# Order of the keys' products, of the layer norm's transposes and of the last ranks in a macaron block

## The chip, the cores and the metric

The kernel runs on one core of a Trainium2 chip. The metric is the time on the device in microseconds (us); the time before is the median of three runs. One further execution was profiled, and all durations, waits and places on the time axis come from it. TensorE is called PE, with its weight loads apart (PEld); VectorE is DVE, ScalarE is ACT, GpSimd is POOL and SyncE is SP.

## The reference

A macaron block on x of shape (2, 1024, 512), all in f32:

```python
x = x + 0.5 * ffn(layernorm(x))      # mixture of 2 experts, top-1 by a router
x = x + attention(layernorm(x))
x = x + 0.5 * ffn(layernorm(x))

def ffn(x):                          # per token: its expert's 512 -> 2048 -> 512
    h = x @ w_fc[e].T; a = square(where(h >= 0, h, 0.5 * h)); y = a @ w_proj[e].T
    # times the router's probability of the chosen expert
```

Attention has 16 heads with keys of 64, values of 128 and 64 slots each. q, k, v, s and a gate g are products of the normalised x with Wq, Wk, Wv, Ws, Wg; s is clipped to +-32. Two recurrences over the tokens keep a state of slots: the first gathers keys by exp(s) and is read by q, a softmax over the slots follows, and the second gathers values by the same weights and is read by that softmax. The result is normalised per head, multiplied with g times sigmoid(g), and goes through Wo.

## The kernel before, in words

**Stages.** The first mixture takes up to about 460 us; attention with its loop runs from about 500 to 1960 us, its last iterations together with the start of the second mixture; the second mixture ends the kernel. Tokens are sorted by expert through DRAM (`xs`): `Mixture.feed` (L248) takes one tile of 128 tokens, its moments and the router's value, and when a group is full (`LAST` groups of 4, 4, 4, 2, 1, 1 tiles in the second mixture) `rank` (L267) finds each token's place. A rank is a few small DVE operations (e L273, bef L280, r0 to pos L286 to L289), two matmuls rp (L282, L283), a square root and a reciprocal (L291, L292), and one indirect store per tile that POOL issues (L294).

**Attention** works on 64 units: for each of 2 batches, for each of 4 groups of 4 heads, 8 chunks of 128 tokens. The loop (L1294 to L1368) runs over i, with unit i as `cur`, i-1 as `mid` and i-2 as `old`. In an iteration stand in this order: steps of projections (keys and slots, values and gates) between the slots' scores of `mid` (ok), the transposes of `old`'s output (`to`), the softmax over the slots (its transposes `ts`, L1149), `transpose_u` (`tu`) and the key state of `mid`, the products for the value state, the transposes of `cur`'s keys and slots (`tk`), queries (pq), outputs (ov) of `mid`, scores (Ap) of `cur`, the output projection (po) of `old`, and the loads for a later group. After the output projection of the last head group the finished tile is fed to the second mixture.

`on_pe` (L947) chains all of these matmuls in the order in which they are written: each is issued after the one before (`att.pe`). The matmuls of the layer norm (ln, L206) and of the ranks (rp, L282 and L283) are not in that chain; the scheduler of the program places them where it finds them.

**Products.** Two neighbouring tiles are projected together by a scheme of seven products in place of eight, with sums of tokens (`X`, L970 to L974) and of weights. `keys_slots` (L1025) is such a generator, run in the even iterations. Its first step makes U (kU: keys' own bank in "pj") and copies it on ACT (kp, L1033), then C, one half of a second bank (kV), to which the key addition on DVE (k, L1052) adds kp. Its second step has the products V (the other half of kV) and U:

```python
            product(V, u.S[:, 0], T1, False)
            p5 = keep(V, "kv")
            product(U, u.S[:, 1], T2, False)
            u2 = keep(U, "ku")
```

`keep` copies a bank to SBUF on ACT. The third step adds a product to V again and forms the slots (E) from it and u2. The steps of `values_gates` (L977), U in "ok" and C, V in "pj", stand between them.

**The layer norm** of attention's input, `layernorm_T` (L185), is a generator over tiles of 128 tokens: load of the tile (xr, two buffers, shared with a copy u2 of `values_gates`; for batch 1 through SP), moments, normalisation on DVE (xr, L203), four transposes into the bank "tr" (one buffer, shared with `tk`, `tu` and `to`), a copy to xnT on ACT (L207), and one yield. In the loop, `next(norm)` is called for batch 0, head group 3 (L1347 and L1348), so that the eight tiles of batch 1 are normalised in iterations 24 to 31.

**Other queues.** POOL multiplies the gate (sg, L1217), forms sums of weights (L548 to L566 in the second mixture), and issues the scatters (L294, L648). SP issues the loads in order, wv (L180) and vgT (L914) among them.

Of the kernel before, what the change touches and what calls it, by code (L numbers as in the profile page):

```python
# [25 lines left out]
NG = H // HG  # L26
# [23 lines left out]
def tile_macaron(  # L50
# [134 lines left out]
    def layernorm_T(src, rows, xT, b, ph):  # L185
        for blk in range(2 * b, 2 * b + 2):
            xT[blk] = large_tile([P, DC, 512], f"xnT{ph}_{blk}")
            for j in range(4):
                nm = f"{ph}_{blk}_{j}"
                xn = work.tile([P, D], F32, tag="xr", name=f"xr{nm}")  # L190
                if b == 0:
                    x = rows[blk][:, j, 0:D]
                else:
                    x = xn
                    nc.sync.dma_start(out=x, in_=src[ts(x1_block(blk) * 4 + j, P), :])
                st = small.tile([P, 6], F32, tag="bnst", name=f"bnst{nm}")
                nc.vector.bn_stats(st, x)
                mv = small.tile([P, 2], F32, tag="mv", name=f"mv{nm}")
                nc.vector.bn_aggr(mv, st)
                rstd = small.tile([P, 1], F32, tag="rstd", name=f"rstd{nm}")  # L200
                nc.scalar.activation(rstd, mv[:, 1:2], AF.Sqrt, bias=eps)
                nc.vector.reciprocal(rstd, rstd)
                nc.vector.tensor_scalar(xn, x, mv[:, 0:1], rstd, ALU.subtract, ALU.mult)  # L203
                tp = ps1.tile([P, DC, P], F32, tag="tr", name=f"ln{nm}")
                for dc in range(DC):
                    nc.tensor.transpose(tp[:, dc, :], xn[:, ts(dc, P)], ident)  # L206
                nc.scalar.copy(xT[blk][:, :, ts(j, P)], tp)  # L207
                yield
# [23 lines left out]
    class Mixture:  # L232
# [3 lines left out]
        def __init__(self, ph, plan, split):  # L236
            self.ph, self.rows, self.split = ph, None, split
            self.passes, self.groups = plan
            self.starts = [sum(self.passes[:j]) for j in range(NPASS)]
            self.e1 = small_t([P, NT], "e1", f"e1{ph}")  # L240
            self.run = small_t([P, NT], "run", f"run{ph}")
            self.before = small_t([P, NT], "bef", f"bef{ph}")
            self.pos = small_t([P, NT], "pos", f"pos{ph}", mybir.dt.int32)

            self.own = small_t([P, NPASS], "own", f"own{ph}")
            self.seen = self.ranked = self.done = 0

        def feed(self):  # L250
            V, i = nc.vector, self.seen
            nm = f"{self.ph}_{i}"
            row = self.rows[i // 4][:, i % 4, :]
            st = small.tile([P, 6], F32, tag="bnst", name=f"bnst{nm}")
            V.bn_stats(st, row[:, 0:D])
            V.bn_aggr(row[:, D : D + 2], st)
            prod = work.tile([P, D], F32, tag="xr" if self.split else "sq", name=f"pr{nm}")
            V.scalar_tensor_tensor(
                prod, row[:, 0:D], row[:, D : D + 1], wd, ALU.subtract, ALU.mult,
                accum_out=row[:, D + 2 : D + 3],  # L260
            )
            self.seen += 1
            if self.seen == self.ranked + self.groups[self.done]:
                self.rank(self.groups[self.done])
                self.done += 1

# [673 lines left out]
    def attention(att, then, then_steps, weight_steps):  # L940
# [84 lines left out]
        def keys_slots(u):  # L1025
            pair = u, units[u.n + 1]
            B11, B21, B22, T1, T2, T3, T4 = att.ks[u.b, u.g]
            a11, a12, a21, a22 = halves(u)
            U = ps2.tile([P, 256], F32, tag="pj", name=f"kU{u.nm}")

            def keep(bank, tag):
                t = work.tile([P, 256], F32, tag=tag, name=f"{tag}{u.nm}", bufs=1)
                nc.scalar.copy(t, bank)  # L1033
                return t

            def key(v):
                v.k = work.tile([P, HG * DK], F32, tag="k", name=f"k{v.nm}")
                return v.k

            def slot(v, bank, other):  # L1040
                v.E = work.tile([P, HG * M], F32, tag="E", name=f"E{v.nm}", bufs=3)
                nc.vector.tensor_tensor(v.E, bank, other, ALU.add)
                nc.vector.tensor_scalar(v.E, v.E, -32.0, 32.0, ALU.max, ALU.min)
                nc.scalar.activation(v.E, v.E, AF.Exp)

            product(U, a11, B11, True)
            p1 = keep(U, "kp")

            bank = ps2.tile([P, 2, 256], F32, tag="pj", name=f"kV{u.nm}")
            C, V = bank[:, 0], bank[:, 1]  # L1050
            product(C, a12, B21, True)
            nc.vector.tensor_tensor(key(u), C, p1, ALU.add)  # L1052
            yield
            product(V, u.S[:, 0], T1, False)
            p5 = keep(V, "kv")
            product(U, u.S[:, 1], T2, False)
            u2 = keep(U, "ku")
            yield
            product(V, u.S[:, 3], B22, False)
            slot(u, V, u2)  # L1060
            yield
            product(U, u.S[:, 2], T3, False)
            slot(pair[1], U, p5)
            yield
            product(U, a22, T4, False)
            nc.scalar.copy(key(pair[1]), U)
            yield
# [78 lines left out]
        def slot_softmax(u):  # L1146
            tp = ps1.tile([P, HG, M], F32, tag="st", name=f"ts{u.nm}")
            for pr in range(NPR):
                on_pe(nc.tensor.transpose,   # L1149
                    tp[:, 2 * pr : 2 * pr + 2, :].rearrange("p h m -> p (h m)"), u.sT[:, pr, :], ident  # L1150
                )
            mx = small.tile([P, HG, 1], F32, tag="mx", name=f"mx{u.nm}")
            nc.vector.tensor_reduce(mx, tp, AX.X, ALU.max)
            u.u = work.tile([P, HG, M], F32, tag="e", name=f"e{u.nm}")
            nc.vector.tensor_tensor(u.u, tp, mx.to_broadcast([P, HG, M]), ALU.subtract)
            nc.scalar.activation(u.u, u.u, AF.Exp)  # L1156
            u.rs = small.tile([P, HG, 1], F32, tag="rs", name=f"rs{u.nm}")
            nc.vector.tensor_reduce(u.rs, u.u, AX.X, ALU.add)
            nc.vector.reciprocal(u.rs, u.rs)
# [19 lines left out]
        def transpose_u(u):  # L1179
            tp = ps1.tile([P, NPR, P], F32, tag="tr", name=f"tu{u.nm}")  # L1180
            for pr in range(NPR):
                on_pe(nc.tensor.transpose, 
                    tp[:, pr, :], u.u[:, 2 * pr : 2 * pr + 2, :].rearrange("p h m -> p (h m)"), ident
                )
            u.uT = work.tile([P, NPR, P], F32, tag="uT", name=f"uT{u.nm}")

            nc.vector.tensor_tensor(u.uT, tp, u.rC, ALU.mult)
# [106 lines left out]
        for i in range(n + 2):  # L1294
# [25 lines left out]
            if mid:  # L1320
                transpose_u(mid)
                update_key_state(mid)
            project("vk", "v")
            if mid:
                slot_weights(mid)
                value_state_products(mid)
# [17 lines left out]
            if old:  # L1344
                project_out(old)
            if cur:
                if cur.g == NG - 1 and cur.b == 0:  # L1347
                    next(norm)  # L1348
                if cur.g == 0 and cur.b and cur.c in (1, 2):
                    att.load_rows(2 * cur.b + cur.c - 1)  # L1350

                if cur.c >= 4 and cur.n + NC < n:
                    v = units[cur.n + NC]
                    if cur.c == 4:
                        att.load_queries(v.b, v.g)
                    elif cur.c == 5:
                        att.load_values_gates(v.b, v.g)
                    elif cur.c == 6:
                        att.load_keys_slots(v.b, v.g)
                    else:  # L1360
                        att.load_outputs(v.b, v.g)
                if cur.g == NG - 1 and cur.b == B - 1:
                    if cur.c == 1:
                        then.lead_pass()
                    elif cur.c >= 3:

                        with tc.issue_after(mid.gated.ins):
                            next(then_steps)  # L1368

    first_mixture = Mixture(0, FIRST, True)  # L1370
    last_mixture = Mixture(2, LAST, False)
# [7 lines left out]
    for ps, ck in ffn(first_mixture, x1_views):  # L1379
        if ps == NPASS - 1 and ck >= 2 and att.rows[ck - 2] is None:  # L1380
            att.load_rows(ck - 2)
        if ps == NPASS - 1 and ck == 3:
            with tc.issue_after(first_mixture.mark_dve.ins):
                next(norm, None)
            if (0, 0) not in att.vg:
                for load in (att.load_values_gates, att.load_keys_slots, att.load_queries, att.load_outputs):
                    load(0, 0)
# [56 lines left out]
```

## Time and profile before

| what | before |
|---|---|
| median of 3 runs | 2368.47 us (2363.77 to 2371.63) |
| profiled execution | 2368.13 us |
| its span | 2366.4 us |
| mean granted clock of TensorE | 0.992 |
| PE busy | 2270.1 us, 10552 matmuls |
| PEld busy | 1566.4 us |
| DVE busy | 1389.4 us |
| ACT busy | 782.9 us |
| POOL busy | 470.8 us |

A line of the timeline has the start in us, the duration in us, the engine, the line of the kernel, the operation, what it writes and reads, and how many were joined; in brackets stands how long the engine was idle before it, and what ended that. A line of the waits has the waiting engine, its tile and line, the releaser, then us in total, how many times and the longest. A line of the windows has the stretch, its length, and for each engine its busy time, then the granted clock of TensorE, the share of DMA and GB/s. Durations of overlapping matmuls do not add up; the distance of their starts does.

### The profile page before, as it was taken

What the parts mean: (1) busy time and instruction counts of PE and PEld (TensorE: products, weight loads), DVE (VectorE), ACT (ScalarE), POOL (GpSimd) and SP (SyncE); (2) the same over time, 40 slices, a digit from 0 to 9 for tenths busy, and PEclk for the clock granted to TensorE, in tenths of its full rate; (3) what the DMA queues carried; (4) which work ended last, traced back from release to release, by engine and by line L of the source; (5) the groups of instructions that cost most, each with busy time, mean ns of one, the idle gap of its engine ahead of it and who ended that gap; (6) DMA issues with size and microseconds to landing.
All of it is one profiled execution on the core that took longest, in us unless ns stands there. A gap on an engine that the chain in (4) does not pass through costs nothing.

```text
span 2366.4 us, 28341 instructions
## 1 busy us (share of the span) xinstructions
PE 2270.1 (96%) x10552; PEld 1566.4 (66%) x10552; DVE 1389.4 (59%) x3116; ACT 782.9 (33%) x1462; POOL 470.8 (20%) x401
## 2 busy tenths in 40 slices
PE   6999999999999999999999999999999989999998
PEld 5686787866656666665556666665665668888865
DVE  6553556557656656756666655655656666666411
ACT  2221222324334333343333343343433322222222
POOL 3613616101101101100101000000001244534000
PEclk9999999999999999999999999999999999999999
DMA  7516435221311411311301110111010104323442
GB/s 285 218 54 241 151 115 221 76 104 45 121 45 63 143 40 54 143 32 37 138 27 58 72 35 15 72 41 35 29 36 31 77 23 152 107 77 120 165 169 98
DMA packets 56938, 222.72 MB, mean 94 GB/s; under 512 B 5983, under 2 KB 13151, under 8 KB 38880
## 3 DMA queue, kind: packets, MB, share of 16 engines
q1 hardware_dynamic: 51232, 203.52, 24.1%
q0 software_dynamic: 5280, 16.85, 1.8%
q8 instruction: 84, 1.38, 0.2%
q14 instruction: 54, 0.44, 0.1%
q10 hardware_dynamic: 288, 0.52, 0.1%
HBM read 189.86 MB, written 31.54 MB: 94 GB/s over the span
## 4 chain that ended last, share of the span: by engine, by line
PE 75%; DVE 13%; issue 6%; ACT 2%; POOL 2%; DMA 1%; SPq 0%; POOLq 0%; DVEq 0%; ACTq 0%
PE U L949 9%; PE oa L673 6%; PE po L949 6%; PE hU L606 6%; PE pq L949 5%; PE o L673 5%; PE V L949 4%; PE kU L949 4%; PE hp L509 4%; PE kV L949 3%; PE hV L606 3%; PE op L728 3%; PE ov L949 3%; PE C L949 2%; DVE rC L1124 2%
## 5 line engine op out<-in xcount | busy, mean ns | idle before, releaser
L1217 POOL TENSOR_TENSOR sg<-sg,ms 128x512 f32<-128x512 f32 x64 | 67.6, 1056 | 1248.6 <-DVE ms L1215 1209.1
L949 PE MATMUL po<-wo,oT 128*128 128x512 f32 x512 | 238.4, 609 | 1.7 <-DVE A L1106 1.7
L949 PEld LDWEIGHTS po<-wo,oT 128*128 128x128 f32 x512 | 92.6, 191 | 102.4 <-issue 93.0
L509 PE MATMUL hp<-xsT,wfc 128*128 128x256 f32 (+1 forms) x768 | 149.8, 350 | 10.3 <-DMA wfc<-in_w_fc_dram 5.6
L509 PEld LDWEIGHTS hp<-xsT,wfc 128*128 128x128 f32 x768 | 128.0, 193 | 33.6 <-issue 13.9
L728 PE MATMUL op<-wp,a 128*128 128x512 f32 x320 | 143.2, 593 | 0.0
L1213 ACT ACT_TABLE_LOAD x64 | 82.1, 1283 | 157.1 <-DVE ms L1212 157.0
L496 DVE SCALAR_TENSOR_TENSOR t<-hp,r 128x256 f32<-128x256 f32 (+1 forms) x96 | 36.3, 378 | 153.7 <-ACT r L495 151.7
L949 PE MATMUL U<-vgT,X 128*128 128x512 f32 x256 | 120.3, 592 | 0.0
L949 PE MATMUL pq<-xnT,wq 128*128 128x512 f32 x256 | 112.5, 592 | 0.0
L1124 DVE RECIPROCAL rC<-CT 128x256 f32<-128x256 f32 x64 | 111.4, 1740 | 0.6
L606 PE MATMUL hU<-xsT,wfc 128*128 128x256 f32 x384 | 100.2, 383 | 0.9 <-ACT e L613 0.9
L728 PEld LDWEIGHTS op<-wp,a 128*128 128x128 f32 x320 | 59.7, 190 | 60.9 <-issue 57.4
L1106 DVE TENSOR_TENSOR A<-Ap,causal 128x256 f32<-128x256 f32 x128 | 53.1, 420 | 54.6 <-PE Ap L949 53.1
L495 ACT ACTIVATE r<-hp 128x256 f32<-128x256 f32 (+1 forms) x96 | 33.3, 348 | 155.3 <-PE hp L509 151.0
L949 PEld LDWEIGHTS pq<-xnT,wq 128*128 128x128 f32 x256 | 47.4, 190 | 53.6 <-issue 53.6
L606 PEld LDWEIGHTS hU<-xsT,wfc 128*128 128x128 f32 x384 | 72.2, 191 | 14.2 <-issue 3.0
L1156 ACT ACT_TABLE_LOAD x63 | 80.8, 1283 | 1.2
L949 PEld LDWEIGHTS U<-vgT,X 128*128 128x128 f32 x256 | 48.6, 190 | 47.6 <-issue 45.9
L995 ACT ACTIVATE th<-sg 128x512 f32<-128x512 f32 x64 | 40.4, 631 | 109.4 <-DVE sg L993 102.4
L1219 DVE TENSOR_TENSOR og<-ov,sg 128x512 f32<-128x512 f32 x64 | 44.2, 690 | 52.0 <-POOL sg L1217 52.0
L1248 ACT ACTIVATE oT<-to,gnh 128x512 f32<-128x512 f32 x64 | 44.0, 687 | 92.4 <-PE to L949 80.7
(296 smaller groups left out, 5087.8 us busy)
## 6 DMA issues: line engine op xcount, KB each, us to landing
wfc<-in_w_fc_dram SPq DMA_DIRECT2D x48, 1024.0 KB, 5.6
wp<-in_w_proj_dram SPq DMA_DIRECT2D x48, 1024.0 KB, 6.9
vgT<-vgs SPq DMA_DIRECT2D x16, 1024.0 KB, 5.3
wv<-in_w_v_dram SPq DMA_DIRECT2D x8, 1024.0 KB, 7.7
ksT<-kss SPq DMA_DIRECT2D x8, 1024.0 KB, 4.9
wo<-in_w_o_dram SPq DMA_DIRECT2D x8, 1024.0 KB, 4.8
xs<-xs SPq DMA_DIRECT2D x6, 1032.0 KB
wks<-in_w_ks_dram SPq DMA_DIRECT2D x24, 256.0 KB, 4.2
```

What stands on the lines that cost most here:

```text
L509: m.mark = nc.tensor.matmul(hp, lhsT=wfc[:, dc * HQ + hc * P : dc * HQ + (hc + 1) * P], rhs=xT[:, dc, :], start=(dc == 0), stop=(dc == DC ...
L606: m.mark = nc.tensor.matmul(bank, lhsT=left[:, d, :], rhs=right[:, d, :], start=start and d == 0, stop=d == 1, skip_group_check=True,)
L673: nc.tensor.matmul(bank[:, t, :], lhsT=left(q)[:, ts(t, P)], rhs=right(q), start=first and q == 0 and (t == 0 or last), stop=last and q == ...
L728: nc.tensor.matmul(ops[j], lhsT=a[hc][:, ts(j, P)], rhs=wp[:, ts(hc, D)], start=(ck == 0 and hc == 0), stop=(ck == NHQ - 1 and hc == HQ // ...
L949: att.pe = op(*args, **kw)
L1106: nc.vector.tensor_tensor(m[:, ts(j, NPR), :], pp, causal[:, 0:NPR, :], ALU.mult)
L1124: nc.vector.reciprocal(u.rC, u.CT)
L1156: nc.scalar.activation(u.u, u.u, AF.Exp)
L1213: nc.scalar.activation(ms, ms, AF.Sqrt, bias=eps, scale=1.0 / DV)
L1217: u.gated = then.gated = nc.gpsimd.tensor_tensor(sg, sg, ms.to_broadcast([P, HG, DV]), ALU.mult)
L1219: nc.vector.tensor_tensor(u.og, op, sg, ALU.mult)
L1248: nc.scalar.activation(u.oT, tp, AF.Copy, scale=gnh)
```

## The change

Four things are changed.

- In the second step of `keys_slots` the product U with its copy ku now stands ahead of V with its copy kv.
- `layernorm_T` gets a second yield between normalisation and transposes. In the loop, after the output projection, the transposes of the tile before are issued behind the last matmul of attention's chain, and then the next tile is normalised (iterations 24 to 31; the last transposes in iteration 32). Ahead of attention one more `next` is called.
- The second mixture's ranks are `deferred`: `feed` no longer ranks, and `settle` does it in each iteration of the loop, (right after `project("vk", "v")`), also behind the last matmul of the chain. After the loop `settle` is called once more.
- Two calls of `on_pe` are broken over lines.

```diff
@@ layernorm_T
                 nc.vector.tensor_scalar(xn, x, mv[:, 0:1], rstd, ALU.subtract, ALU.mult)
+                yield
                 tp = ps1.tile([P, DC, P], F32, tag="tr", name=f"ln{nm}")
@@ class Mixture, __init__
             self.seen = self.ranked = self.done = 0
+            self.deferred = not split
@@ feed
             self.seen += 1
-            if self.seen == self.ranked + self.groups[self.done]:
+            if not self.deferred:
+                self.settle()
+
+        def settle(self):
+            while self.done < len(self.groups) and self.seen >= self.ranked + self.groups[self.done]:
                 self.rank(self.groups[self.done])
                 self.done += 1
@@ keys_slots
             yield
+            product(U, u.S[:, 1], T2, False)
+            u2 = keep(U, "ku")
             product(V, u.S[:, 0], T1, False)
             p5 = keep(V, "kv")
-            product(U, u.S[:, 1], T2, False)
-            u2 = keep(U, "ku")
             yield
@@ the loop of attention
             project("vk", "v")
+            with tc.issue_after(att.pe.ins):
+                then.settle()
             if mid:
                 slot_weights(mid)
@@
             if cur:
-                if cur.g == NG - 1 and cur.b == 0:
+                if (cur.b, cur.g) == (0, NG - 1) and cur.c or (cur.b, cur.g, cur.c) == (1, 0, 0):
+                    with tc.issue_after(att.pe.ins):
+                        next(norm)
+                if (cur.b, cur.g) == (0, NG - 1):
                     next(norm)
@@ after the loop
+        then.settle()
@@ ahead of attention, in the last pass of the first mixture
             with tc.issue_after(first_mixture.mark_dve.ins):
+                next(norm, None)
                 next(norm, None)
```

More of the change, by code (lines that the diff above doesn't have):

```diff
@@ L1148, in slot_softmax @@
             for pr in range(NPR):
-                on_pe(nc.tensor.transpose,
+                on_pe(
+                    nc.tensor.transpose,
                     tp[:, 2 * pr : 2 * pr + 2, :].rearrange("p h m -> p (h m)"), u.sT[:, pr, :], ident
@@ L1181, in transpose_u @@
             for pr in range(NPR):
-                on_pe(nc.tensor.transpose,
+                on_pe(
+                    nc.tensor.transpose,
                     tp[:, pr, :], u.u[:, 2 * pr : 2 * pr + 2, :].rearrange("p h m -> p (h m)"), ident
```

## The prediction

> **What bounds the kernel now.** I read the page first: the share of each engine, and the chain that ended last.
>
> ```profile
> PE 2270.1 (96%) x10552; PEld 1566.4 (66%) x10552; DVE 1389.4 (59%) x3116; ACT 782.9 (33%) x1462; POOL 470.8 (20%) x401
> ...
> PE 75%; DVE 13%; issue 6%; ACT 2%; POOL 2%; DMA 1%; SPq 0%; POOLq 0%; DVEq 0%; ACTq 0%
> ```
>
> TensorE is the bound, and the change neither adds nor removes a matmul. It can only move the idle time of PE, so the next view is what PE waited for, in attention above all.
>
> ```profile
> PE rp L282 <- DVE e L273: 17.2, 4, 12.6
> PE kV L949 <- DVE k L1052: 14.0, 21, 1.8
> ...
> PE hC L606 <- DVE e L1155: 6.3, 1, 6.3
> ```
>
> The second row is the keys' V product waiting for the key addition. Of the first row 12.6 us is the first mixture's start, which the change leaves alone. The timeline of one even iteration shows the wait in place:
>
> ```profile
> 630.17 0.41 DVE L1052 TENSOR_TENSOR k<-kV,kp 128x256 f32<-128x256 f32 x1
> ...
> 630.64 0.73 PEld L949 LDWEIGHTS kV<-ksT,X 128*128 128x128 f32 x4 [0.78 <-DVE k L1052]
> 630.64 1.13 PE L949 MATMUL kV<-ksT,X 128*128 128x256 f32 x4 [0.53 <-DVE k L1052]
> ...
> 631.61 1.03 PE L949 MATMUL kU<-ksT,X 128*128 128x256 f32 x4
> 631.81 0.37 ACT L1033 COPY kv<-kV 128x256 f32<-128x256 f32 x1 [3.37 <-PE kV L949]
> ...
> 632.47 0.60 PE L949 MATMUL to<-ident,og 128*128 128x128 f32 x4
> ...
> 632.91 0.38 PE L949 MATMUL ts<-ident,sT 128*128 128x128 f32 x2
> ...
> 633.13 1.03 PE L949 MATMUL kV<-wks,X 128*128 128x256 f32 x4
> ```
>
> V (630.64) shares a bank with C, which the addition reads, so it waits until 630.58. The kU product at 631.61 needs nothing from that addition. Next come the places where the layer norm's and the rank's own matmuls stand in PE's order:
>
> ```profile
> 1077.67 0.66 PE L206 MATMUL ln<-ident,xr 128*128 128x128 f32 x4 [0.86 <-DVE xr L203]
> ...
> 1079.00 0.65 PE L949 MATMUL to<-ident,og 128*128 128x128 f32 x4 [0.68 <-ACT xnT L207]
> ```
>
> ```profile
> 1098.29 1.13 PE L949 MATMUL kV<-ksT,X 128*128 128x256 f32 x4 [1.78 <-DVE k L1052]
> ```
>
> ```profile
> 1845.49 0.39 PE L282 MATMUL rp<-e,strict 128*128 128x4 f32 x2 [1.61 <-DVE e L273]
> ```
>
> Here PE waits for the normalised tile, then for the bank "tr" that ln, tk, tu and to share, then for a key addition that stands on DVE behind the norm, and for a rank. All are waits in a chain that has no slack.
>
> **Keys' U ahead of V.** In the trace a 256-column matmul starts 216 ns after the one before it, so U's four take 864 ns. I measured from the last ok<-A,E matmul to the first matmul of `to`. With no wait (iterations 10, 18, 42, 50, 58) it is 2.033 us; in 17 other even iterations between 4 and 56 it is 2.51 to 2.80, because V starts 0.68 to 0.97 after that matmul instead of 0.20. The 17 excesses add to 10.4 us. U's 864 ns covers each of them whole, so they vanish. What is late next is V's third step at 633.13, which needs the kv copy. Now U and `to`, `ts` stand between: 945 ns of slack. Afterwards only `to` and `ts` do (4 and 2 transposes of 108 ns, 648 ns): slack 945 - 864 = 81 ns. The trace has a near row: U<-vgT,xnT starts with its releaser done 84 to 86 ns before and loses 79 ns, while with 183 ns nothing is lost. Behind it on PE stands the whole chain. I take 79 ns in 28 pairs, 2.2 us (bounds 0 and 28 x 0.37, one more ACT copy). In pair 0 no `to` and `ts` stand there, and V's third step waits about what V waited before (0.75), so it counts nothing. Sum: 10.4 - 2.2 = **8.2 us**.
>
> **Layer norm's transposes.** The distance of iterations (tk to tk) repeats with a period of eight: 19.65, 25.43, 19.22, 19.00, 20.76, 25.87, 20.68, 19.00 us. Over that pattern units 25 to 32, where a tile of batch 1 is normalised in each, are longer by 0.44, 0.94, 2.42, 2.08, 1.98, 2.87, 2.42, 2.15: 15.3 us. Afterwards the tile is normalised an iteration ahead and its four transposes follow the output projection: no wait for DVE, `tr` free. The transposes stay, 4 x 108 + 58 ns = 0.49 us each, 3.9 us for eight. The pattern itself holds V waits of 0.60, 0.66 and 0.66 for pairs 28, 30 and 32 that U removes too: +1.9. The key addition is still late behind the norm on DVE there: V waited 1.95 us in pairs 28 and 32, minus 0.86 leaves about 1.1 us over the three. V's third step costs 0.3. Sum 15.3 - 3.9 + 1.9 - 1.1 - 0.3 = **11.9 us**. The norm's first stage on DVE (bn_stats, xr, 0.54 us each) is only moved; its cover is the 41% of DVE that is idle, and exposed it would cost 8 x about 1.4 us (bn_stats 0.69, its sum-up 0.16, xr 0.54). The new orderings chain matmuls of PE among themselves, which it runs in order anyway, so they add no wait by themselves.
>
> **Ranks.** Deferred until after the step that contains V, two rp matmuls and their wait leave the place ahead of V. Rank at iteration 34: its unit is 21.53 against 19.22, 2.3 us, of which bef/rp work and a smaller wait stay; I take **1.0**. Iteration 62: 24.55 against 21.1 us, and 0.6 of V's regular wait; less 1.5 that stays, **2.5**. In iteration 60 PE waited 1.94 us ahead of the second mixture's lt, behind the same addition; U fills 0.87 of it, and with the third step's share I take **1.3**.
>
> Here a rule speaks about these stalls. After each, the granted clock fell:
>
> ```profile
> 1847.50:1850.50 3.00, 3.00 (x12) 2.52 (x12) 0.64 (x4) 0.48 (x2) 1.51 (x2) 0.50 0.11 40
> ```
>
> The 0.50 is the granted clock. It stood 3.41 us after stalls of 1.8 to 2.1 us at 1792, 1845 and 1881, costing 1.7 us each, but not after two of 1.95 at 1098 and 1204. The Trainium skill (TensorE: Matmul & The Clock Gate, "Why this matters for your kernels") wants no idle gap over about 3 us: by it such stalls cost no clock and shortening them returns only themselves. By the row two of them return 1.7 more each. I count the one at 1847 within iteration 62 and leave the other for the low end.
>
> **The tail.** After the loop's ranks, POOL runs weight sums without a gap, and a DVE operation sits through them:
>
> ```profile
> 1898.68 7.30 DVE L498 SCALAR_TENSOR_TENSOR t_1b<-hB 128x512 f32<-128x512 f32 x1
> ```
>
> ```profile
> 1899.30 1.27 POOL L551 TENSOR_TENSOR wfc<-wfc 128x512 f32<-128x512 f32 x1
> ```
>
> ```profile
> 1906.46 1.19 PE L606 MATMUL hC<-xsT,wfc 128*128 128x256 f32 x2 [6.32 <-DVE e L1155]
> ```
>
> Ordinarily t_1b takes 0.68. The rule in SBUF — State Buffer ("SBUF: two separate sides") is that a DVE operation with two SBUF inputs and a GpSimd one exclude each other for one whole instruction. That would be one POOL sum, 1.27 us; the row has five back to back, 6.6 us more. I take the row. Deferring the ranks moves their scatters (L294) past these sums, so the train is the same eight sums closed up, ending about 2.4 us earlier. Half-clock time after it (10.24 us) may shrink. Bounds: -2 (both scatters of rank 12, 0.99 us each, in the path) to +5 (most of the 6.32); I take **1.7**, nearer the train's 2.4. The last ranks' scatters stand ahead of other sums on POOL; those waited 10.4 us for PE before, more than a scatter (0.99 us), so nothing is charged.
>
> **Sum.** 8.2 + 11.9 + 1.0 + 2.5 + 1.3 + 1.7 = 26.6 us. From the profiled execution, 2368.13 (span 2366.4), this is 2341.5; it lies 0.3 under the median of runs, 2368.47. I say **2341**.
>
> **Rivals.**
> *Keys' gain given back.* The 81 ns of V's third step rest on ACT copying kv at once. If one more ACT operation like the ku copy (372 ns) comes between, V's third step waits 0.37 - 0.08 = 0.29 more in 28 pairs, 8.1 us: 2350. For it: nothing else stands between. Against: ACT is busy 33%, and ku is copied before V ends. Chance 0.17.
> *Clock and tail return more.* The half clock at 1793 and part of the 10.24 us go (1.7 + 3 to 5 us): 2334. For it, the three rows above; against, the two stalls that cost nothing. Chance 0.15.
> *It doesn't do what it says*: the waits move whole to the next operation, for DVE's work is the same and the additions come no earlier. Within 3 us of before, 2366. Against: iterations without the wait run 2.033, so nothing else stops them. Chance 0.05.
> *Slower: loads held on SP.* SP issues in order. The x tiles of batch 1 (xr) now wait for their buffer's transposes an iteration later, and two of them stand ahead of the loads of wv and vgT, issued at 1117.64, 1127.95 and 1134.02. I expect those at about 1143, and U<-wv needs them at 1167.63; with 7 to 8 us to land, 17 us are left. A hold of d costs d - 17: one iteration of 21.5 more gives 4.5, two 26, and it decides against the change from d = 44. At three, 64.5 us, the time is 2341 + 47 = 2388. Nothing I see holds them more than one. Chance 0.03.
>
> **How the numbers follow.** The sum as worked has 0.60, around 2341. The low end, 2334, takes in the clock case; the high end, 2351, the gain given back. The last two cases, 0.08, and some spread lie outside. A measurement of this kernel can tell 0.3%, 7 us, from no change: below 2361 is faster. Only the fourth case is the same, only the fifth slower. Faster 0.94, same 0.03, slower 0.03.
>
> **What would show it.** Right: kV<-k waits all but gone from the PE rows, with the step from ok<-A,E to `to` at 2.0 to 2.1 us in regular pairs; ln waits gone, units 25 to 32 within 0.7 us of the pattern; rp after V with waits under 1 us in 34 and 62. Wrong: a new row kV<-kv with 0.3 us or more each; ln or lt waiting for `tr`; U<-wv or U<-vgT waiting for a DMA; an hC or hV wait in the tail longer than 6.3.

## The result and the profile after

The changed kernel takes 2335.56 us (median of four runs, 2334.97 to 2335.80) against 2369.09 of the kernel before in the same comparison: a ratio of 0.9861, with a 95% interval of 0.9844 to 0.9878. Its profiled execution has a span of 2334.1 us, 32.3 less than before, and a mean granted clock of 0.996. From the page, busy times and the chain:

```profile
PE 2260.4 (97%) x10552; PEld 1560.6 (67%) x10552; DVE 1386.8 (59%) x3116; ACT 781.2 (33%) x1462; POOL 471.8 (20%) x401
...
PE 80%; DVE 10%; issue 5%; DMA 2%; ACT 1%; POOL 1%; SPq 0%; POOLq 0%; another core or an unknown queue 0%; DVEq 0%; ACTq 0%
```

The same matmuls have a larger share of a shorter chain, and DVE's share fell from 13% to 10%. What PE waited for now (total, times, longest):

```profile
PE rp L288 <- DVE e L279: 12.8, 1, 12.8
...
PE to L955 <- DVE og L1227: 3.6, 4, 2.1
...
PE kV L955 <- DVE k L1058: 3.2, 6, 0.8
```

Of rp only the first mixture's start is left; V's wait fell from 14.0 us in 21 places to 3.2 in 6. The wait of `to` for og grew from 1.0 us in 2 places to 3.6 in 4, up to 2.1 us long. The timeline of the iteration shown before:

```profile
629.94 1.13 PE L955 MATMUL kU<-ksT,X 128*128 128x256 f32 x4
630.06 0.41 DVE L1058 TENSOR_TENSOR k<-kV,kp 128x256 f32<-128x256 f32 x1
...
630.91 1.03 PE L955 MATMUL kV<-ksT,X 128*128 128x256 f32 x4
...
631.97 0.37 ACT L1039 COPY kv<-kV 128x256 f32<-128x256 f32 x1 [0.49 <-PE kV L955]
...
632.42 1.10 PE L955 MATMUL kV<-wks,X 128*128 128x256 f32 x4
```

U runs while the addition ends, and V follows without a wait. V's third step (the last row) starts 80 ns after the kv copy ends (632.34), about the 81 ns foreseen.

To see where 32.3 us come from I laid both traces side by side, by the distance of each iteration's first tk transpose to the next. "Tail" is what follows the last of them:

| place | foreseen gain, us | measured, us |
|---|---|---|
| regular iterations 1 to 24 and 35 to 59 | 8.2 | 9.7 |
| iterations 25 to 33, beside the layer norm | 11.9 | 5.6 |
| iteration 34 | 1.0 | 0.8 |
| iteration 60 | 1.3 | 0.0 |
| iteration 62 | 2.5 | 3.4 |
| tail | 1.7 | 13.1 |
| up to the first tk | 0 | -0.3 |
| sum | 26.6 | 32.3 |

The sum is near, but two terms are far off in opposite directions: that they nearly cancel is luck. They are what the experiments are for. Each group of the norm's transposes now stands where the prediction put it, right behind the output projection and without a wait:

```profile
1063.93 3.70 PE L955 MATMUL po<-wo,oT 128*128 128x512 f32 x8
1067.46 0.60 PE L207 MATMUL ln<-ident,xr 128*128 128x128 f32 x4
```

Nevertheless iteration 31 is longer than before, 23.99 us against 21.42, though it has no rank and no norm wait. The timeline of POOL there, and then PE's:

```profile
1154.12 0.96 POOL L300 DMA_INDIRECT xs<-x,pos  x1 [0.30 <-issue]
1155.09 0.20 POOL L142 COPY x<-toki 128x4 int32<-128x4 int32 x1
1161.47 0.19 POOL L142 COPY x<-toki 128x4 int32<-128x4 int32 x1 [6.18 <-DMA xs<-x,pos]
1161.61 1.03 POOL L1225 TENSOR_TENSOR sg<-sg,ms 128x512 f32<-128x512 f32 x1
```

```profile
1163.52 0.63 PE L955 MATMUL to<-ident,og 128*128 128x128 f32 x4 [2.12 <-DVE og L1227]
```

Behind the deferred rank's scatters on POOL stand two copies of token numbers into row tiles. The second copy waits 6.18 us for the scatters to land, and the gate's multiplication sg stands behind it; og and `to` follow. The order on POOL was the same before, but there scatters and copies were done nine microseconds ahead of the next gate:

```profile
1155.56 1.04 POOL L294 DMA_INDIRECT xs<-x,pos  x1 [0.30 <-issue]
1160.06 0.32 POOL L142 COPY x<-toki 128x4 int32<-128x4 int32 x2 [3.46 <-PE kU L949]
1169.63 1.04 POOL L1217 TENSOR_TENSOR sg<-sg,ms 128x512 f32<-128x512 f32 x1 [9.25 <-DVE ms L1215]
```

Deferred, the scatters have moved up against the gate, which starts 12.0 us after the iteration's first tk in place of 8.5. The windows show what the clock does then (last columns: granted clock, DMA share, GB/s):

```profile
1161.20:1164.40 3.20, 0.82 (x5) 0.42 (x4) 1.72 (x5) 0.23 (x2) 1.18 (x2) 1.00 0.60 190
1164.60:1167.80 3.20, 3.20 (x6) 1.65 (x7) 3.10 (x9) 2.12 (x3) 0.00 (x0) 0.50 0.31 120
```

In the tail the DVE operation that had taken 7.30 us is short. Before, it began (1898.68) in the issue of a scatter with five sums behind it; now the rank's first scatter is issued after the last sum. The first row is of before, the others are of after:

```profile
1898.28 0.99 POOL L294 DMA_INDIRECT xs<-x,pos  x1 [0.30 <-issue]
```

```profile
1876.25 1.75 DVE L504 SCALAR_TENSOR_TENSOR t_1b<-hB 128x512 f32<-128x512 f32 x1
```

```profile
1885.18 1.02 POOL L300 DMA_INDIRECT xs<-x,pos  x1
```

```profile
1879.62 1.10 PE L612 MATMUL hV<-T,S 128*128 128x256 f32 x4 [2.35 <-DVE hA L644]
```

The last row is PE's longest wait there; it stands in place of the 6.32 us for hC.

### The profile page after: what moved, and what is told of

It is laid out like the page before. It is cut to its first block, busy times and chain, and to the rows that moved or that the text cites. A ratio compares the mean times of both kernels' runs of the same rounds, so it can differ in the third digit from the quotient of the medians.

```text
span 2334.1 us, 28356 instructions
## 1 busy us (share of the span) xinstructions
PE 2260.4 (97%) x10552; PEld 1560.6 (67%) x10552; DVE 1386.8 (59%) x3116; ACT 781.2 (33%) x1462; POOL 471.8 (20%) x401
## 4 chain that ended last, share of the span: by engine, by line
PE 80%; DVE 10%; issue 5%; DMA 2%; ACT 1%; POOL 1%; SPq 0%; POOLq 0%; another core or an unknown queue 0%; DVEq 0%; ACTq 0%
PE U L955 9%; PE po L955 8%; PE oa L679 6%; PE hU L612 6%; PE V L955 5%; PE pq L955 5%; PE o L679 5%; PE kU L955 4%; PE kV L955 4%; PE ov L955 4%; PE hV L612 3%; PE hp L515 3%; PE op L734 3%; PE C L955 3%; PE ok L955 2%
```

## The experiments

**Theory** after the result: keys and norm bring what the waits say. The tail comes from the fourth rank's two scatters leaving the train of POOL's sums, so that t_1b no longer sits through it. The loss in iteration 31 is POOL held by the copies. **Rival**: the tail is shorter only because everything ends earlier and the half-clock stretches fall elsewhere; and the loss in 25 to 33 comes from the norm's moved stage on DVE. The clock records of the traces give the time at half clock. Work there takes twice as long: in the stretch at 1792.91 us of the kernel before, 256-column matmuls start 427 ns apart in place of 216. A stretch thus costs about half its length, and less where PE waits in it (iteration 60 lost 1.44 us to one of 3.41). "Span less clock" below is the span minus half of the time at half clock, and a gain "less clock" is worked out from it. For the kernel before it is 2366.4 - 39.65 / 2 = 2346.6, for the changed one 2334.1 - 21.32 / 2 = 2323.4: 9.2 us of the 32.3 are clock.

**Keys alone.** From the changed kernel, the norm's split and the deferral undone:

```diff
-            self.deferred = not split
+            self.deferred = False
...
                 nc.vector.tensor_scalar(xn, x, mv[:, 0:1], rstd, ALU.subtract, ALU.mult)
-                yield
...
-                    with tc.issue_after(att.pe.ins):
-                        next(norm)
```

> Only U ahead of V in the keys' second step; the norm's transposes and the ranks stand as before. Theory: of the 32 us, the order of the products gives 9.7 in regular pairs and some 2 to 3 in the pairs beside the layer norm (V stalls of 1.95 us less U's 0.86); the tail behind the last iteration is left as it was, because what shortens it is that the ranks' scatters leave POOL: 2368 - 12.5 = about 2356. Rival: the tail gets shorter merely because the loop ends at another time and the half-clock stretches fall elsewhere; then this alone shortens the tail too, towards 2345.

Measured: 2349.85 us, ratio 0.9930 (0.9907 to 0.9953). Regular iterations gained 9.5 us, 25 to 33 only 1.1, the tail 3.3. Less clock, the span fell by 14.9, the tail by 1.8. The median lies between the two expectations; the tail's stall is unchanged (t_1b 7.30 us), so the rival is not borne out by the trace, but the clock moved by 4.9 us in this one execution, 1.5 of them in the tail. Iteration 34 gained 0.7 and iteration 62 2.4, with their ranks where they were.

**Norm alone.** The order of keys' products and the deferral undone:

```diff
-            self.deferred = not split
+            self.deferred = False
...
-            product(U, u.S[:, 1], T2, False)
-            u2 = keep(U, "ku")
             product(V, u.S[:, 0], T1, False)
             p5 = keep(V, "kv")
+            product(U, u.S[:, 1], T2, False)
+            u2 = keep(U, "ku")
```

> Only the layer norm's transposes behind the output projection. Theory: iterations 25 to 32 lose 15.3 us over the regular pattern, 3.9 of it are the transposes themselves and about 2 are waits of V behind the key addition that stay: about 9 less, 2359, with no half-clock stretch at 1164 us, since no rank holds POOL there. Rival: the norm's moved stage on DVE is what made these iterations gain only 5.6 us with the whole change: then about 2363.

Measured: 2354.05 us, ratio 0.9957 (0.9943 to 0.9971). Iterations 25 to 33 gained 5.3, with 31 shorter by 1.98 and no half clock at 1164. Two other half-clock stretches appeared, at 1144 us in this part and at 1233 us in iteration 34, each about 1.7 us of cost; the ones that iterations 60 and 62 had before did not come, and these gained 1.4 and 1.7 though nothing in them was changed. Less clock the span fell by 8.9, about the 9 expected; the median is 5 us under the 2359 expected.

**Ranks alone.** Keys and norm undone, the deferral left.

```diff
                 nc.vector.tensor_scalar(xn, x, mv[:, 0:1], rstd, ALU.subtract, ALU.mult)
-                yield
...
-            product(U, u.S[:, 1], T2, False)
-            u2 = keep(U, "ku")
             product(V, u.S[:, 0], T1, False)
             p5 = keep(V, "kv")
+            product(U, u.S[:, 1], T2, False)
+            u2 = keep(U, "ku")
```

> Only the ranks deferred. Theory: the tail gains about 13 us (the DVE operation t_1b no longer sits through five POOL sums, and the half-clock stretches that follow go), iteration 62 gains 3.4, iteration 31 loses 2.6 since the four scatters and the copies behind them hold POOL while the gate waits: 2368 - 14 = about 2354. Rival (tail by chance of time): tail within 2 us of before, 2366.

Measured: 2359.70 us, ratio 0.9976 (0.9969 to 0.9983), between the theory's 2354 and the rival's 2366. The tail gained 11.4, iteration 62 2.7; iteration 31 lost 4.6 and iteration 34 1.7, each with a half-clock stretch. Less clock the whole gain is 4.8 us, that of the tail 6.0. t_1b took 1.75 us. The tail's rival is out: with the loop no shorter than before, the tail is shorter all the same.

**Keys and norm, ranks as before.**

```diff
-            self.deferred = not split
+            self.deferred = False
```

> The whole change without deferred ranks. Theory: the tail is as before, iteration 31 has no wait for the gate: 2368 - 12.5 - 8.5 = about 2347. Rival (tail by chance of time): the tail shorter here too, 2336 or less.

Measured: 2339.17 us, ratio 0.9887 (0.9867 to 0.9907): not the 2347 of the theory, nor the rival's 2336. The sizes were off: with both changes iterations 25 to 33 gained 10.1, more than the 6.4 of the two alone (1.7 of the difference are the stretch at 1144 us), iteration 60 1.4 and 62 2.4. The tail gained 3.8, of which 3.3 are clock. Its stall stood as before:

```profile
1869.93 7.29 DVE L504 SCALAR_TENSOR_TENSOR t_1b<-hB 128x512 f32<-128x512 f32 x1
```

So the deferral on top of the other two brought little (ratio 0.9861 against 0.9887, with intervals that overlap): in the traces its tail is shorter by 9.2 us (5.1 less clock), and its iteration 31 longer by 4.6.

**The changed kernel again**, as a mark.

> The changed kernel once more, as the mark for the three others: about 2335.6. The half-clock stretches of 3.41 us lie on a grid of 3.413 us whose phase no kernel sets; if they follow from where a stall falls on that grid, some of them stand elsewhere in this execution, or are missing, with the same waits.

Measured: 2333.44 us, ratio 0.9857 (0.9841 to 0.9872). `to` waited 1.71 us for og in iteration 31, and this time no half-clock stretch followed: 21.91 us in place of 23.99. One appeared at 1877.6 instead. Of the 2.1 us between the two, 0.4 are the wait and the rest the clock. Part of what two executions of one kernel differ by is thus where a stall falls on the clock's grid.

**Only late ranks deferred**, from iteration 40 on, by a line at the head of the loop:

```diff
-            self.deferred = not split
+            self.deferred = False
...
+            then.deferred = i >= n // 2 + NC
```

> Ranks deferred only from iteration 40 on, so that the first two stand as before the change and the later ones as after it. Theory: the wait of `to` for og in iteration 31 (2.1 us, and the half clock behind it) goes, since POOL's scatters come early again and the gate doesn't wait behind the copies; the tail keeps what it gained: 4 to 5 us less than the changed kernel, about 2331. Rival (the stall comes from the norm's moved stage, not from POOL): no difference, 2335.5.

Measured: 2329.96 us, ratio 0.9836 (0.9823 to 0.9849); iterations 25 to 33 gained 10.1 over the kernel before, the wait for og is gone. That is 3.5 us under the changed kernel beside it, though the intervals overlap. The rival, the norm's stage, is out: it stands here as in the changed kernel, and the wait is gone.

**Only the scatters late.** Ranks computed in their old places; from the third on their scatters are issued at the deferred place.

```diff
+            if self.hold:
+                self.held.append(scatter)
+            else:
+                scatter()
...
+            then.hold = i >= n // 2 + NC
...
-                then.settle()
+                then.release()
```

> Ranks computed where they stood before the change, matmuls included; only the scatters of the third rank and later are issued at the deferred place. Keys and norm as changed. Theory: what shortens the tail is the two scatters leaving the train of POOL's sums, so t_1b takes about 1.7 us in place of 7.3 and the tail is 8 to 9 us shorter than with keys and norm alone: about 2330. Rival: the rp matmuls' place on PE does it; then t_1b takes 7.3 and the time is 2339.

Measured: 2336.24 us, ratio 0.9867 (0.9852 to 0.9883), not 2330. No DVE operation sat through the train any more, yet PE waited in the next place:

```profile
1874.76 1.34 PE L623 MATMUL hV<-xsT,S 128*128 128x256 f32 x4 [2.99 <-DVE hB L648]
```

hB waited behind three Q sums on DVE, each lengthened by a wait for one POOL sum (1.23 to 1.48 in place of 0.41). The tail, less clock, is 2.9 us shorter than before, against 6.1 with late ranks deferred whole and 0.6 with keys and norm alone. In these single traces the scatters' place thus explains about half of the tail's gain; the other half came only when the rank's small operations and matmuls moved too. Why was not taken apart further.

**Copies late.** The changed kernel, with the two copies held behind the gate of the iteration:

```diff
-                    att.load_rows(2 * cur.b + cur.c - 1)
+                    with tc.issue_after(mid.gated.ins):
+                        att.load_rows(2 * cur.b + cur.c - 1)
```

> The changed kernel with the two copies of token numbers held behind the gate's multiplication on POOL. Theory: what held POOL at 1155 to 1161 us was the second copy, waiting for the scatters to land; four scatters of 1.26 us remain and end before the gate is ready: `to` waits 0 to 0.5 us in iteration 31, 4 to 5 us less than the changed kernel, about 2331. Rival: the scatters themselves hold POOL; less than 1.5 us gained.

Measured: 2331.24 us, ratio 0.9845 (0.9830 to 0.9859). That is 2.2 us under the changed kernel beside it, not 4 to 5, and the intervals overlap. In the trace the gate runs 3.5 us earlier in its iteration, 8.5 us after the first tk as before the change:

```profile
1157.56 1.04 POOL L1225 TENSOR_TENSOR sg<-sg,ms 128x512 f32<-128x512 f32 x1 [3.04 <-DVE ms L1223]
```

It no longer waits for POOL, and iteration 31 is 19.44 us, against 23.99 and 21.91 in the two executions of the changed kernel. PE has no wait for og left in this stretch; what remains between 1035 and 1240 us is V's:

```profile
PE kV L955 <- DVE k L1058: 2.8, 5, 0.8
```

The copy, not the scatters themselves, held the gate.

**The feed an iteration later**, on top of the last two versions:

```diff
             if u.g == NG - 1:
-                then.feed()
+                if u.b:
+                    then.feed()
+                else:
+                    due.append(u)
@@ behind the second project("k", "v")
+            while due:
+                due.pop()
+                then.feed()
```

> The changed kernel, the copies late on POOL, and for batch 0 the feed of a finished tile to the second mixture moved into the next iteration, behind the step with U, so that the router's product (pr, 0.74 us on DVE) stands behind the key addition. Theory: the V waits of 0.63 to 0.98 us that stay in iterations 26 to 34 come from pr and its aggregate standing ahead of the key addition; five of them go, 3 to 3.5 us less than with the copies alone: about 2328. Rival: og, not pr, sets when the addition starts; less than 1 us.

> Ranks deferred only from iteration 40 on, with the same move of the feed. The early ranks' matmuls stand ahead of V in iterations 30 and 34 and now come after a later pr: V's waits in 26, 28, 32 go (about 2 us), those in 30 and 34 stay or grow by up to 0.9 each: 2328 to 2330. Which of the two is the faster says whether the first two ranks are better deferred, once the copies and the key addition are out of the way.

Measured: 2332.15 us, ratio 0.9848 (0.9835 to 0.9860), and 2333.50 us, 0.9850 (0.9837 to 0.9864). Neither is below the version without the move (0.9845 and 0.9836), and in the second's trace iterations 25 to 33 are 1.0 us longer. The trace of the first tells why: in 28, 32 and 34 moments and pr still stood ahead of the key addition on DVE, since a place in the program binds only where an order is written; only in iteration 30 does V start earlier (0.31 us late in place of 0.71). The question was not put by these kernels.

**The feed bound behind the key addition.**

```diff
-            nc.vector.tensor_tensor(key(u), C, p1, ALU.add)
+            att.added = nc.vector.tensor_tensor(key(u), C, p1, ALU.add)
@@ behind the second project("k", "v")
...
+                with tc.issue_after(att.added.ins):
+                    then.feed()
```

> As the version with the copies late on POOL, and the whole feed of a finished tile (moments and router product) held behind the key addition on DVE, which the move into the next iteration alone had not done in 26, 28 and 32. Theory: V's waits of 0.63 to 0.98 us in the even iterations 26 to 34 go, since without moments and pr the addition starts at least 0.7 us earlier: 3 us less than with the copies alone. Rival: og, which waits for POOL, still stands ahead and sets the addition's start; less than 1 us.

> The mark beside it: the changed kernel with the copies late, about 2331, with V's waits of 0.63 to 0.98 us in iterations 26 to 34 as before.

Measured: 2328.14 us, ratio 0.9839 (0.9826 to 0.9852), beside 2329.52, 0.9850 (0.9836 to 0.9863), of the mark. In the trace four of the five waits are gone. Iteration 26, which has no feed ahead of it and waits behind og, keeps 0.68, and 34 has a new wait, for the kv copy:

```profile
PE kV L955 <- DVE k L1058: 0.5, 1, 0.5
PE kV L955 <- ACT kv L1039: 0.3, 1, 0.3
```

Iterations 25 to 34 are 2.7 us shorter than in the mark. At the medians the difference is 1.4 us, and the intervals overlap, so the runs do not separate these two versions. Against the changed kernel (0.9857 and 0.9861) the version with the bound feed, at 0.9839, has the lower ratio, as the one with late ranks has (0.9836); these intervals overlap too, while the traces show iteration 31 in each shorter than in the two executions of the changed kernel, by 4.6 and by 2.5 us.

## Why the prediction was right, and where only its sum was

The forecast of faster, and the range, held; the median lies 5.4 us under the predicted 2341, near the low end. That the sum came so near is in part luck: 9.2 of the 32.3 us are clock, most of it not in the sum, and a term 6.3 us too high stands beside one 11.4 too low. One sign that the prediction named failed: units 25 to 32 were to lie within 0.7 us of the pattern, and 31 lies 5.0 above. By its own steps:

- **Keys' U ahead of V**: the mechanism and both sizes hold. Each waiting pair gained its excess less 75 to 80 ns, as the 81 ns of slack told; a pair without a wait lost 70 to 80 ns (iterations 10 and 18: 19.22 to 19.29). The term was 8.2 and measured 9.7: I had left pair 24 out (0.69) and charged V's third step in 28 pairs, where this part has 23; pair 42 lost another wait of 0.3.
- **Layer norm's transposes**: waits gone as foreseen, 0.4 to 0.5 us per tile of transposes paid. The step that failed is "leaves about 1.1 us over the three": V starts 0.63, 0.71 and 0.63 us late in 28, 30 and 32 (2.0 in all), with 0.69 in 26 and 0.98 in 34, because the key addition stands behind og and the router's product. (The row of 2.8 us in 5 places counts only PE's idle part.) The size was a slip of mine too: 1.95 less 0.86 is 1.1 in each of two pairs, 2.2 over both. The version with the bound feed shows that all but the one in 26 come from the feed (moments and pr), which I had not put into the sum.
- **Ranks, scatters**: "so nothing is charged" failed. I had looked only at POOL's queue in the tail, and not at the first rank, where the scatters and the copies that wait for their landing stand ahead of the gate: 4.6 us in iteration 31 with the half clock after it, 2.5 in the execution without. Copies late and late ranks both took it back. This and V's waits are the gap between 11.9 and 5.6.
- **Iterations 34 and 62**: near in size (1.0 and 2.5 foreseen, 0.8 and 3.4 measured), but I had credited both to the deferral and, in 62, to the clock. Keys alone, with the ranks in place, already gains 0.7 in 34. In 62 norm alone gains 1.7 because no half clock came; less this, keys alone gains 0.7 and ranks alone 1.0.
- **Iteration 60**: 1.3 foreseen, 0.0 measured. The first wait of lt fell from 1.94 us (before, the first row) to 0.88, as worked out, but U no longer stands between the groups of lt, and those now wait for ACT's copy of the group before:

```profile
1792.44 0.71 PE L482 MATMUL lt<-ident,xn 128*128 128x128 f32 x4 [1.94 <-DVE xn L476]
```

```profile
1776.57 0.66 PE L488 MATMUL lt<-ident,xn 128*128 128x128 f32 x4 [0.88 <-DVE xn L482]
...
1779.44 0.63 PE L488 MATMUL lt<-ident,xn 128*128 128x128 f32 x4 [0.73 <-ACT xsT L489]
1780.80 0.63 PE L488 MATMUL lt<-ident,xn 128*128 128x128 f32 x4 [0.73 <-ACT xsT L489]
```

  I named V's third step as what is late next and did not ask the same of lt. A half-clock stretch came in iteration 60 of both kernels. Where it didn't, the iteration took 26.06 us, with U ahead (copies late, keys and norm) as without (norm alone): U brought nothing here, and the 1.4 us that those kernels gained are the clock's.
- **The tail**: right in kind, mis-sized: 1.7 against 13.1. Half-clock time behind the last tk fell from 22.6 to 7.7 us, 7.5 us of gain; the other 5.6 are stalls, above all hC's 6.32 us, in whose place hV waits 2.35. I took the row of 7.30 us for t_1b as what stays and moved only its end. With the scatters gone it takes 1.75 us, its own 0.69 and a wait of 1.06, less than one POOL sum; that agrees with the Trainium skill (SBUF — State Buffer, "SBUF: two separate sides"), a lock for one instruction. In the four kernels with 7.30 us t_1b began 0.4 us into the issue of a scatter, with five sums queued behind it; in the ten others it took 1.4 to 1.8. Why it did not get in between those sums was not found. The row was true, and held for a situation that the change removes.
- **Rivals**: the clock and tail case was the nearest in time (2334), for its reason in the tail but not in iteration 60. V's third step never waited for more than its 80 ns, but for pair 0 (0.46 us). Loads behind xr held nobody: no PE wait for wv or vgT appears.

## What to carry to other kernels

When a step is moved later on one engine, follow every instruction that it issues, and on each queue ask what stands behind it at each of the places where it runs; here one rank of several paid for the move. A wait that is filled should be followed by two questions: what is late next, and whose cover was taken away with the work that filled it. Stalls that leave most of one step of the clock's grid idle (here 3.41 us, 60% or more) cost their own time and then may cost half a step more, so the value of removing them is not their length alone.

## What the runs showed of the hardware

All half-clock stretches of an execution start on one grid of 3.413 us (233.02, 407.10 and 1792.91 us of the kernel before differ by 51 and 406 such steps) and last one or more steps. From the starts of the matmuls, at 427 ns for 512 columns, I worked out the idle share of PE in each step. In the 14 profiled executions, between 30 and 2300 us, 58 stretches began; every one followed a step that was idle for 60% or more, and no step idle for more than 64% was without one; between 60 and 64% both occur. It is the idle time of the whole step that goes with it, not the length of one stall. Ahead of the stretch at 1792.91 us of the kernel before there is one stall of 2.1 us; ahead of the one in iteration 60 of the changed kernel (at 1782.3) no stall is over 0.9 us, but several share a step, idle by 71%. And a stall that a step's edge cuts in two can stay without one: the stall of iteration 31 left one step idle by 83% in one execution, 51% in the other. The Trainium skill (TensorE: Matmul & The Clock Gate, "Why this matters for your kernels") warns of gaps over about 3 us; these runs put the mark lower. A kernel that fills a stall with matmuls, to move a step across the mark on purpose, was not tried.

In three places a DVE operation with two inputs in SBUF did not get in between POOL's sums behind an indirect store: t_1b in the tail (7.30 us in each of the four kernels that had that order), a Q sum at about 400 us (3.55 us in place of 0.42) and t_1b at about 105 us (2.89 us; it began 0.2 us after the issue had ended). The last two stand in all 14 executions. It is not so for every such operation: at about 265 us t_0b began 0.24 us into such an issue, with a sum next on POOL, and took its usual 0.69 us. What decides was not found. Elsewhere none was found that lost more than 1.35 us, about one sum.
